# Layer norms written by ScalarE as a scale and a per-row bias, in an adaLN Mamba block on one Trainium2 core

## The chip, the core and the metric

The kernel runs on one core of a Trainium2 chip. The time is the device time in microseconds (us) of one execution; the number that counts is the median of several runs. Engines are named as the profile names them: PE is TensorE (matmuls; PEld are its weight loads), DVE is VectorE, ACT is ScalarE, POOL is GpSimd, and SP is the engine whose queue issues most DMAs. Each engine works through its own queue in order; an instruction that waits holds up all that stand behind it on that engine.

## The reference: what is computed

The input x has 4 batches of 512 rows with 512 features. Six modulation vectors per batch come from a small conditioning input c. The block then computes, in fp32:

```python
mod = (_silu(L0_c) @ L0_wmod).reshape(L0_c.shape[0], 6, 1, -1)
h = _layernorm(x, axis=-1) * (1 + ca) + sa
x = x + ga * _L0_attn_ref(h, ...)
h = _layernorm(x, axis=-1) * (1 + cb) + sb
x = x + gb * _L0_ffn_ref(h, L0_ffn_weight, L0_ffn_bias)
```

`_layernorm` is `(x - m) / sqrt(v + 1e-5)` with the mean m and the variance v of a row. `_L0_attn_ref` is a Mamba2 layer: an input projection, a causal convolution of width 4 with silu for x, B and C, a chunked state-space scan over chunks of 128 rows with 64 heads of 16 features, a gate silu(z), and an output projection. `_L0_ffn_ref` is one 512 x 512 matmul with a weight that is reduced to its signs and one scale per output.

## The kernel before

**Tiling.** The 2048 rows are worked on in 8 "halves" h of 256 rows (two to a batch), each in two chunks c of 128 rows. A half has a front and, per chunk, four units (h, c, gp) of 16 heads, and a tail.

**Front of a half.** `load_x` (L75) brings two tiles of 128 x 512. `f_norm` (L307) normalises them with `layer_norm` (L289) under the name a0 to a7; the result is written over the tiles. `f_hT` (L335) turns them on TensorE (`turned_x`, L325, matmuls phT at L330) and ScalarE applies the modulation (L347) into hT. `f_dt` (L353) computes the time steps, mostly on VectorE, and writes sums, exponentials and reciprocals to DRAM. `f_B`, `f_C`, `f_x` run projections (matmuls at L434), a ScalarE step (L450), three VectorE taps of the convolution (L454), tanh on ScalarE (L458) and a VectorE product (L459). `f_z` projects the gate (L434, pp_z; ScalarE L516 and L520, VectorE L522). `f_turned_sums` (L415) turns the sums (pn, L419 to L427).

**A unit.** SP's queue loads the sums of its heads, broadcast (L541, L542). ScalarE takes 16 exponentials of 128 x 128 (L549). VectorE multiplies them by the masked product of C and B (gm L621, L625). TensorE multiplies with x (py, L212 and L215), VectorE and GpSimd add the rest (L666, L671 or L674, L672) and multiply by the gate (L675), and GpSimd prepares the next state (xd, L679).

**Tail of a chunk.** `tail1` (L729): 8 matmuls po (L739) with wout, then on VectorE the gate (L742), the sum with x (L743) into x2, `layer_norm` under the name f{h}_{c} from x2 into t, and on GpSimd the addition of the bias row to x2 (L745). `tail2` (L751): four transposes ph (L757) and four ScalarE activations h (L759). `tail3` (L765): the feed-forward matmuls pf (L775), VectorE L777 and L778, and the store.

**Layer norm** (L289). For each tile VectorE takes the statistics (L295, L296), adds epsilon to the variances (L297); GpSimd raises them to the power of -0.5 (L298), and VectorE computes (t - mean) times rs in one instruction per tile (L300). The a norms have two tiles, the f norms one.

**Start.** `f_first` (L311) does a0 and the first modulation rows. In the first half the kernel also loads the late modulation weights and works them out (`late_mods`, L233, VectorE L243 to L260, with two rows of gates stored over SP's queue at L262), loads wout over the same place (L265), and loads the feed-forward weight in four pieces fw (L272), whose sums and signs VectorE (L274, L277) and ScalarE (L278) take.

**Order.** The lists FRONT, FIRST and SECOND and the steps of the tails fix in which order the program states its work: per step first the fronts, then the tails, then the unit's matmuls and the loads and exponentials of the unit two ahead. The framework's scheduler then makes each engine's queue from it at build time, by order of statement and by when it thinks an instruction's inputs are there. `issue_after` and `glued` pin some matmuls. PSUM tiles with the tag "mm" share 5 places, which the projections, the transposes and the tails take in turn.

Of the kernel before, what the change touches and what calls it, by code (L numbers as in the profile page):

```python
# [11 lines left out]
F32 = mybir.dt.float32  # L12
AF = mybir.ActivationFunctionType
ALU = mybir.AluOpType
AX = mybir.AxisListType
PSUM = bass.MemoryType.PSUM
P = 128
# [23 lines left out]
def adaln_mamba_block(  # L41
# [15 lines left out]
    nc = tc.nc  # L57
# [13 lines left out]
    wk = ctx.enter_context(tc.tile_pool(name="wk", bufs=2))  # L71
# [27 lines left out]
    mhalf = keep.tile([P, 2], F32, name="mhalf")  # L99
# [189 lines left out]
    def layer_norm(tiles, name, into=None):  # L289
        n = len(tiles)  # L290
        st = wk.tile([P, n, 6], F32, tag=f"st{n}", name=f"st_{name}")
        mv = wk.tile([P, n, 2], F32, tag=f"mv{n}", name=f"mv_{name}")
        rs = wk.tile([P, n], F32, tag=f"rs{n}", name=f"rs_{name}")
        for j, t in enumerate(tiles):
            nc.vector.bn_stats(st[:, j, :], t)  # L295
            nc.vector.bn_aggr(mv[:, j, :], st[:, j, :])  # L296
        nc.vector.tensor_scalar(rs, mv[:, :, 1], EPS, None, ALU.add)  # L297
        nc.gpsimd.tensor_tensor(rs, rs, mhalf[:, :n], ALU.pow)  # L298
        for j, t in enumerate(tiles):
            nc.vector.tensor_scalar(  # L300
                into[j], t, mv[:, j, 0:1], rs[:, j : j + 1], ALU.subtract, ALU.mult
            )


# [2 lines left out]
    def f_norm(h):  # L307
        H[h]["xn"] = xs_of.pop(h)
        layer_norm(H[h]["xn"], f"a{h}", H[h]["xn"])
# [419 lines left out]
    def tail1(h, c):  # L729
        b = h // HPB  # L730
        x2 = tails[h, c]
        po = ps.tile([P, DM], F32, tag="mm", name=f"po_{h}_{c}")
        last = (h, c) == (NHALF - 1, 1)
        for g in range(NKI):
            if last and g == NKI - 2:

                with tc.issue_after(last_po.ins):
                    tail2(h, 0)
            last_po = mm(po, H[h]["z"][g // 2][:, g % 2, c * CH : (c + 1) * CH], wout[:, g, :],  # L739
                         start=(g == 0), stop=(g == NKI - 1))  # L740
        t = wk.tile([P, DM], F32, tag="t", name=f"t_{h}_{c}", bufs=1)
        nc.vector.tensor_mul(t, po, gates[b][:, 0, :])  # L742
        nc.vector.tensor_add(x2, x2, t)  # L743
        layer_norm([x2], f"f{h}_{c}", [t])
        nc.gpsimd.tensor_add(x2, x2, gates[b][:, 2, :])  # L745
        tails[h, c] = (x2, t)
        if last:
            with tc.issue_after(last_po.ins):
                tail3(h, 0)
# [156 lines left out]
```

## Time and profile before

| what | value |
|---|---|
| median of 3 runs | 733.64 us (733.6 to 734.45) |
| the profiled execution | 737.38 us |
| its span in the profile | 735.7 us |
| mean granted clock of TensorE | 0.993 |
| instructions | 15007 |

The profile is of one execution, whose time is the span and 1.68 us around it. A line of the list of instruction groups gives the line number, engine, operation, written and read tiles with their shape, the count, the busy time in us and the mean duration of one in ns, then the engine's idle time just before them and what ended most of it. A line of a timeline gives the start, the duration, the engine, the line and the operation, and in brackets the idle time before it and its releaser. The durations of some groups that bear on the change:

| line and engine | what | count | mean ns of one |
|---|---|---|---|
| L295 DVE | statistics of an f tile | 16 | 688 |
| L296 DVE | their mean and variance | 16 | 171 |
| L297 DVE | variance plus epsilon, f (a) | 16 (8) | 143 (222) |
| L298 POOL | power, f (a) | 16 (8) | 560 (1055) |
| L300 DVE | the norm applied, x tiles | 16 | 654 |
| L745 POOL | bias row added to x2 | 16 | 1342 |
| L549 ACT | an exponential into decay | 960 | 395 |

### The profile page before, as it was taken

To read this page: it belongs to the slowest core of one execution; us is meant where nothing else is said; L and a number is where in the kernel's file an instruction comes from. 1 tells how busy PE (TensorE), PEld (TensorE's weight loads), DVE (VectorE), ACT (ScalarE), POOL (GpSimd) and SP (SyncE) were. 2 spreads that over 40 slices of the span, in tenths; PEclk is the share of its full clock that TensorE was granted. 3 is DMA by queue.
4 is the path that set the end of the run, shared out by engine and by line. 5 is a ranking of instruction groups with operands and counts; after the bars stand their busy time and mean duration, and the time that the engine had idled before them with its cause. 6 is when DMAs were issued, how large, how long until landed. Compare 5 with 4: busy or idle time off the path is not lost.

```text
span 735.7 us, 15007 instructions
## 1 busy us (share of the span) xinstructions
PE 700.4 (95%) x5196; PEld 500.8 (68%) x5196; DVE 599.5 (81%) x1170; ACT 522.0 (71%) x1507; POOL 254.8 (35%) x297
## 2 busy tenths in 40 slices
PE   6999979899999999999999999999999999999997
PEld 3786746666677666677677666776667866677754
DVE  3869888876998678986899768996799867996995
ACT  2467658748696697785976787865968768788941
POOL 4021323444243332343223342433414332333652
PEclk9999989999999999999999999999999999999999
DMA  8991693535555256444644256552564537457720
GB/s 279 328 291 41 204 208 85 135 98 142 127 132 144 63 155 137 102 115 102 159 116 130 53 116 168 142 137 53 140 132 114 130 86 176 116 150 151 142 69 29
DMA packets 119067, 99.24 MB, mean 135 GB/s; under 512 B 73984, under 2 KB 97152, under 8 KB 118992
## 3 DMA queue, kind: packets, MB, share of 16 engines
q1 hardware_dynamic: 117808, 96.39, 52.3%
q0 software_dynamic: 896, 1.38, 0.7%
q8 instruction: 41, 0.67, 0.4%
q10 hardware_dynamic: 288, 0.52, 0.2%
q14 instruction: 34, 0.28, 0.1%
HBM read 92.47 MB, written 5.79 MB: 134 GB/s over the span
## 4 chain that ended last, share of the span: by engine, by line
PE 65%; ACT 16%; DVE 9%; DMA 4%; issue 4%; POOL 1%; SPq 1%; ACTq 0%; DVEq 0%; POOLq 0%
PE po L739 14%; PE pp_x L434 11%; PE pp_z L434 10%; ACT decay L549 9%; PE pp_C L434 7%; PE pp_B L434 5%; PE pf L775 3%; PE py L212 2%; PE py L215 2%; DVE decay L625 2%; ACT h L759 2%; DVE u_x L454 2%; DMA fw<-in_ffn_w 2%; ACT win L549 2%; PE gy L215 2%
## 5 line engine op out<-in xcount | busy, mean ns | idle before, releaser
L549 ACT ACTIVATE decay<-decay,st 128x128 f32<-128x128 f32 x960 | 293.9, 395 | 4.2 <-DMA decay<-sums_d 3.7
L625 DVE SCALAR_TENSOR_TENSOR decay<-decay,gm 128x1024 f32<-128x1024 f32 x120 | 160.8, 1341 | 50.3 <-ACT decay L549 47.2
L434 PE MATMUL pp_x<-hT,win 128*128 128x259 f32 x512 | 120.7, 390 | 7.3 <-DVE u_C L454 7.3
L434 PE MATMUL pp_z<-hT,win 128*128 128x256 f32 x512 | 118.1, 383 | 0.0
L434 PEld LDWEIGHTS pp_x<-hT,win 128*128 128x128 f32 x512 | 96.9, 193 | 25.2 <-ACT decay L549 7.7
L739 PE MATMUL po<-wout,z 128*128 128x512 f32 x256 | 113.8, 595 | 0.0
L434 PEld LDWEIGHTS pp_z<-hT,win 128*128 128x128 f32 x512 | 94.3, 189 | 16.3 <-issue 3.5
L675 POOL TENSOR_TENSOR z<-yt,z 128x256 f32<-128x256 f32 x62 | 62.9, 1015 | 76.1 <-DVE yt L674 57.8
L454 DVE SCALAR_TENSOR_TENSOR u_x<-pp_x,cw,u_x 128x256 f32<-128x256 f32 x192 | 83.6, 474 | 1.3 <-ACT u_x L450 0.7
L739 PEld LDWEIGHTS po<-wout,z 128*128 128x128 f32 x256 | 47.5, 190 | 53.1 <-issue 52.4
L672 POOL TENSOR_TENSOR yt<-yt,xs 128x256 f32<-128x256 f32 x46 | 41.4, 899 | 106.3 <-DVE yt L671 78.6
L507 POOL TENSOR_TENSOR xs<-u_x,rr 128x512 f32<-128x512 f32 x32 | 42.7, 1334 | 79.2 <-DVE u_x L459 61.3
L516 ACT ACTIVATE uz<-pp_z,zb 128x256 f32<-128x256 f32 x64 | 27.5, 470 | 59.0 <-PE pp_z L434 59.0
L215 PE MATMUL py<-decay,xpad 128*32 128x128 f32 x1680 | 66.3, 276 | 0.0
L434 PE MATMUL pp_B<-hT,win 128*128 128x259 f32 x256 | 63.5, 396 | 2.7 <-ACT decay L549 1.9
L434 PE MATMUL pp_C<-hT,win 128*128 128x259 f32 x256 | 59.6, 384 | 1.1 <-DVE u_x L454 1.1
L775 PE MATMUL pf<-bwT,h 128*128 128x512 f32 (+1 forms) x136 | 59.0, 578 | 1.4 <-ACT h L759 1.3
L434 PEld LDWEIGHTS pp_B<-hT,win 128*128 128x128 f32 x256 | 47.4, 193 | 14.5 <-ACT decay L549 3.1
L450 ACT ACTIVATE u_x<-pp_x,cb,cw 128x256 f32<-128x256 f32 x64 | 35.3, 560 | 30.5 <-PE pp_x L434 30.4
L434 PEld LDWEIGHTS pp_C<-hT,win 128*128 128x128 f32 x256 | 47.8, 189 | 9.4 <-PE pn L424 1.4
L679 POOL TENSOR_TENSOR xd<-xpad,st 128x256 f32<-128x256 f32 x48 | 34.1, 727 | 55.8 <-PE pst L215 28.3
L212 PE MATMUL py<-decay,xpad 128*32 128x128 f32 x240 | 47.4, 279 | 3.2 <-issue 2.2
(157 smaller groups left out, 1080.9 us busy)
## 6 DMA issues: line engine op xcount, KB each, us to landing
decay<-sums_d SPq DMA_DIRECT2D x120, 256.0 KB
decay<-sums_d SPq DMA_DIRECT2D x120, 128.0 KB
rr<-r_d SPq DMA_DIRECT2D x64, 128.0 KB
e<-e_d SPq DMA_DIRECT2D x96, 64.0 KB
win<-in_w_inT SPq DMA_DIRECT2D x4, 1024.0 KB
xr<-in_x SPq DMA_DIRECT2D x16, 256.0 KB
res<-o SPq DMA_DIRECT2D x15, 256.0 KB
x<-in_x SPq DMA_DIRECT2D x14, 256.0 KB
```

The source lines that it names most:

```text
L212: first = products[0]()
L215: product()
L434: last = mm(pm, win[:, k, col : col + P], H[h]["hT"][:, k, lo:], start=(k == 0), stop=(k == NK - 1))
L450: nc.scalar.activation(u[:, j, :], pm[:, KS - 1 :], AF.Identity, bias=cb[:, t : t + 1], scale=cw[:, t, KS - 1 : KS])
L454: nc.vector.scalar_tensor_tensor(u[:, j, :], pm[:, k : k + T], cw[:, t, k : k + 1], u[:, j, :], ALU.mult, ALU.add)
L507: nc.gpsimd.tensor_tensor(xs, xc, rr, ALU.mult)
L549: nc.scalar.activation(ets[r][:, i, :], ets[r][:, i, :], AF.Exp, bias=H[h]["st"][:, hd : hd + 1], scale=-1.0)
L625: nc.vector.scalar_tensor_tensor(ets[r], ets[r], 1.0, bc_mid(gm[:, r, :], HPG), ALU.min, ALU.mult)
L672: ew.tensor_add(t, t, xs)
L675: ew.tensor_mul(zg, t, zg)
L739: last_po = mm(po, H[h]["z"][g // 2][:, g % 2, c * CH : (c + 1) * CH], wout[:, g, :], start=(g == 0), stop=(g == NKI - 1))
L775: mm(pf, h2[:, k, :], bwT[:, k, cols], start=(k == 0), stop=(k == NK - 1))
```

## The change

In `layer_norm` the norm a0 keeps the former way. For all other norms the sum (t - mean) rs is written as rs t + (-mean rs): VectorE negates the means into a new small tile nm (its tag has the pool's two buffers), GpSimd multiplies nm by rs after the power, and ScalarE writes each tile as an Identity activation with rs as per-row scale and nm as per-row bias. Nothing else is edited.

```diff
         nc.vector.tensor_scalar(rs, mv[:, :, 1], EPS, None, ALU.add)
+        if name == "a0":
+            nc.gpsimd.tensor_tensor(rs, rs, mhalf[:, :n], ALU.pow)
+            for j, t in enumerate(tiles):
+                nc.vector.tensor_scalar(
+                    into[j], t, mv[:, j, 0:1], rs[:, j : j + 1], ALU.subtract, ALU.mult
+                )
+            return
+
+        nm = wk.tile([P, n], F32, tag=f"nm{n}", name=f"nm_{name}")
+        nc.vector.tensor_scalar(nm, mv[:, :, 0], -1.0, None, ALU.mult)
         nc.gpsimd.tensor_tensor(rs, rs, mhalf[:, :n], ALU.pow)
+        nc.gpsimd.tensor_mul(nm, nm, rs)
         for j, t in enumerate(tiles):
-            nc.vector.tensor_scalar(
-                into[j], t, mv[:, j, 0:1], rs[:, j : j + 1], ALU.subtract, ALU.mult
+            nc.scalar.activation(
+                into[j], t, AF.Identity, bias=nm[:, j : j + 1], scale=rs[:, j : j + 1]
             )
```

## The prediction

> **What bounds the kernel now.** I read the page first (busy time, the 40 slices, the chain), then the list of waits, then TensorE's timeline for its gaps, and last the timelines of the engines around each layer norm.
>
> ```profile
> PE 700.4 (95%) x5196; PEld 500.8 (68%) x5196; DVE 599.5 (81%) x1170; ACT 522.0 (71%) x1507; POOL 254.8 (35%) x297
> ...
> PE 65%; ACT 16%; DVE 9%; DMA 4%; issue 4%; POOL 1%; SPq 1%; ACTq 0%; DVEq 0%; POOLq 0%
> ```
>
> TensorE is busy for 95% of the span and holds 65% of the chain that ended last. Added up over its timeline, the gaps before a matmul come to 31.7 us, 6.2 of them ahead of the first matmul and 5.4 in one piece at 94.05 us. So no edit on VectorE or ScalarE can win more than a part of these gaps, and work added to either costs only where TensorE already waits for that engine or nearly does. The chain holds ScalarE for 16% and VectorE for 9%, so the engine that gets the work is the one that sets the end more often.
>
> The layer norms show in the waits. The columns are the time waited in all, the number of waits, the longest:
>
> ```profile
> ACT uz L516 <- PE pp_z L434: 59.0, 15, 9.1
> ...
> POOL xr L745 <- DVE t L300: 6.8, 11, 0.7
> ...
> DVE t L300 <- POOL rs_f L298: 12.8, 16, 1.4
> ```
>
> VectorE's queue stands 0.8 us on average (12.8/16) behind GpSimd's pow before each L300 of a feed-forward row; and ScalarE has long idle stretches, but they lie where it waits for the z projection, not everywhere.
>
> **The change, part by part.** Changed are the norms a1 to a7 (two tiles each) and the 16 norms of feed-forward rows (one tile each): 30 L300 instructions leave VectorE, and 30 activations, 23 tiny multiplies on VectorE (nm = -mean) and 23 tiny multiplies on GpSimd (nm times rs) come. The rows that price them (mean ns of one after the bar):
>
> ```profile
> L516 ACT ACTIVATE uz<-pp_z,zb 128x256 f32<-128x256 f32 x64 | 27.5, 470 | 59.0 <-PE pp_z L434 59.0
> L450 ACT ACTIVATE u_x<-pp_x,cb,cw 128x256 f32<-128x256 f32 x64 | 35.3, 560 | 30.5 <-PE pp_x L434 30.4
> L300 DVE TENSOR_SCALAR t<-xr,mv_f,rs_f 128x512 f32<-128x512 f32 x16 | 11.5, 719 | 12.8 <-POOL rs_f L298 12.8
> L278 ACT ACTIVATE sw<-sw,alpha 128x512 f32<-128x512 f32 x4 | 2.9, 723 | 3.0 <-DVE sw L277 3.0
> ```
>
> *The activation*: L278 is the same function, shape and memory with a per-row scale: 723 ns. L450 differs from L516 in a per-row scale beside the per-row bias, 90 ns. So 723 + 90 = 0.81 us each, 30 x 0.81 = 24.4 us more ScalarE busy time. Neighbours overlap: eight exponentials of 395 ns take 2.44 us together, 0.305 each, 0.09 less than one alone; so an activation takes 0.81 - 0.09 = **0.72 us** of a busy queue.
>
> *VectorE*: L300 has a median of 546 ns (719 is the mean, stretched where GpSimd works beside it). Both L300 groups are 11.5 + 9.8 us busy; less a0's two (1.6) that is 19.7 us out, up to 16.2 us of waits out with them (12.8 for the rows, 3.4 for x). In come 16 x 143 + 7 x 222 ns = 3.8 us by the rows of L297, the same operation and shapes. These stand behind L297, so the pow starts no later.
>
> *GpSimd's multiply* is not in the trace. From below: the 128x2 memset of L100, 92 ns. From above: the pow of the same shape, 558 ns. A tensor-tensor of L672 takes 0.72 us for 256 columns and one of L745 1.28 us for 512 where nothing disturbs them, which leaves 0.17 us for no columns; I take 0.2 us. L745 now waits for the activation instead of L300 and comes some 0.5 us later; behind it on GpSimd stand yt L672, z L675 and xd L679, on an engine with 65% idle.
>
> The new wait is that of the activation on GpSimd. Behind it on ScalarE's in-order queue stand the exponentials L549, u L450, th L458, h L759. TensorE waits for h (PSUM is handed on), VectorE for the exponentials.
>
> Now by place. **Norms f of the second 128 rows of a half** (six places: 165, 251, 338, 425, 512, 598 us): ScalarE idles before uz L516, for example 6.29 us until 253.24. The pow there ends at 251.64; plus 0.2 and 0.81 gives 252.7, before 253.24. Cost 0. **a2 to a7**: the two activations push ScalarE by 1.4 us and idle stretches of about 6 us follow at once; the transposes of x come 20 us later. Cost 0. If the order took that cover away, the price would be that of the next group.
>
> **Norms f of the first 128 rows**, in ScalarE's busiest stretch. At 292 us:
>
> ```profile
> 292.04 0.55 DVE L300 TENSOR_SCALAR t<-xr,mv_f,rs_f 128x512 f32<-128x512 f32 x1 [1.39 <-POOL rs_f L298]
> ...
> 292.56 1.20 ACT L450 ACTIVATE u_x<-pp_x,cb,cw 128x256 f32<-128x256 f32 x2
> ...
> 296.52 1.48 ACT L759 ACTIVATE h<-ph,modT 128x128 f32<-128x128 f32 x4
> ...
> 298.06 2.02 PE L434 MATMUL pp_B<-hT,win 128*128 128x259 f32 x8 [0.24 <-ACT h L759]
> ```
>
> ScalarE has no gap from 290.2 to 298.4, and TensorE waits for h at its end. What is put into that queue ahead of h comes out on TensorE. The stall of 1.39 us that VectorE loses can reappear on ScalarE: none of it if the activation stands behind the eight exponentials, all of it plus 0.2 if ahead. I take 0.3 us, nearer to none, since the exponentials there cover most of it; so d = 0.72 + 0.3 = **1.0 us** per such place (ends: 0, when it lands in a gap, and 1.7).
>
> The sum:
> - 292, 465, 638 us, alike: 3 x 1.0 = +3.0 (0 to 5.1).
> - 206 and 379: here the chain runs through L300, and TensorE waits 0.57 for u_x L454, which goes; but pn L419 waits for h, and would end at 213.40 + 1.0 instead of 213.97: +0.43 each, +0.9 (-1.1 to +2.3).
> - 552: TensorE waits 0.44 for h: +1.0 (0 to 1.7).
> - 685: ScalarE is full from 679 to 706 with the exponentials of the last half and thz L520 holds up VectorE and then py: +1.0 (0 to 1.7).
> - 118: the queue of VectorE is full until 138 and two gaps, 0.78 and 1.94, wait for it. It gains 0.42 of stall and 0.46 of work, loses 0.14: -0.75 (-1.0 to 0). ScalarE's results are there 1.5 us early or more, which hides d.
> - a1, 74 us: TensorE waits 1.02 for x. Two activations behind uz, xpad, thz: +0.5 (0 to 1.3).
> - The gap of 5.36 at 94: VectorE stands 1.49 and 0.32 us for fw, issued at 82.26 in SP's queue, which earlier stood 3.7 us for ab L260; that stood behind a1's L300. Without these, ab is some 2.8 us earlier, then fw and the gap: at most the 1.81 that VectorE waits, I take -1.5 (-1.8 to 0).
> - The end, 726.5: multiply 0.2, activation 0.81 for 0.55: +0.46 (0.4 to 0.9). At 718.8 matmuls of po hide it.
>
> 3.0 + 0.9 + 1.0 + 1.0 - 0.75 + 0.5 - 1.5 + 0.46 = **+4.6 us**. The profiled execution took 737.38 us, 1.68 more than its span of 735.7, and would be 742.0. The median of the runs, 733.64, is 3.7 below it; the same step there gives **738.2 us**.
>
> A rule speaks against the change itself: the Trainium skill, "ScalarE: Activation LUTs", section "Rules for kernel authors", gives add and multiply to VectorE, not ScalarE. The rows bear it out for one instruction (0.81 against 0.55). By the rule alone each of the eight saturated places and the end would pay 0.26, 2.4 us in all; the trace says that the price is not the difference but the place in the queue.
>
> **The rivals.**
> - *VectorE's relief decides* (faster). The place is VectorE's queue around the first-row norms and a1; the price is what the sum grants at its lower ends: -1.8, -1.0, -1.1 and the end's +0.4 = -3.5, **730.1 us**. It decides from the point where d falls below about 0.2 us, that is, where the build places the activations into ScalarE's short waits for u_C and pp_x (1.19 us before 289.69). For it: 36 us leave VectorE's queue (19.7 + 16.2), and ScalarE's waits for th_C on u_C, 24.2 us, are VectorE's lateness. Against: TensorE's gaps that VectorE ends hold some 15 us, most of them before 140 us.
> - *A wash*: ScalarE's 200 us of idle time takes all 30, and gains and losses cancel: **733.6 us**. For it: 22 of the 30 sit in idle stretches already.
> - *The stall moves whole*: the build puts the activation ahead of the eight exponentials at each saturated place, ScalarE stands for the full lag of the pow, GpSimd's L745 behind it, and z and yt behind that. Upper ends: 5.1 + 2.3 + 1.7 + 1.7 + 1.3 + 0.9 - 0 = +13, **746.6 us**.
> - That it doesn't do what it says: the instructions do move, but the build orders every queue anew, so places far from any norm may shift by parts of a microsecond either way; the trace can't price that, and the range carries it.
>
> **How the numbers follow.** Forecast 0.48, relief 0.27, wash 0.15, whole stall 0.10. Within 0.2% of 733.64 (1.5 us) is about what can't be told from no change: that is the wash. Slower by more: 0.48 + 0.10 = 0.58; faster by more: 0.27. The forecast's own range is 735.2 to 742. The range for 8 in 10 takes in the relief down to its end, 730.0, and the forecast with the beginning of the whole stall, up to 745.0.
>
> **What would show it.** Right: ScalarE 546 us busy, VectorE about 583, TensorE's still 700; activations of t near 0.81 us, GpSimd's multiply near 0.2; wider TensorE gaps after h L759 near 298, 471, 645 us; an earlier fw and a gap below 4 us near 94. Wrong: the gaps after h unchanged because the activations sit in waits; TensorE's gaps for u_C and u_x gone altogether; or fw no earlier.

## The result and the profile after

| | before | after |
|---|---|---|
| median of the runs beside each other | 734.05 us (733.6 to 735.5, 4 runs) | 756.36 us (755.84 to 757.5, 4 runs) |
| ratio, with its 95% interval | 1 | 1.0303 (1.0283 to 1.0322) |
| profiled execution, its span | 737.38, 735.7 us | 756.03, 754.3 us |
| mean granted clock of TensorE | 0.993 | 0.989 |

The changed kernel is 3% slower, 22 us, where 4.6 us were forecast. 756.36 us lies above the whole range. The two profiled executions are only 18.6 us apart, since the one of before was slower than the median of its kernel. In the kernel after, the lines below the edit move by 11 (L434 is L445, L549 is L560, L759 is L770); the activation is L311, the power L308, GpSimd's multiply L309.

First the page of the kernel after: busy time of each engine, and the shares of the chain that ended last.

```profile
PE 705.6 (94%) x5196; PEld 502.6 (67%) x5196; DVE 583.2 (77%) x1163; ACT 544.1 (72%) x1537; POOL 270.4 (36%) x320
...
PE 59%; ACT 16%; DVE 15%; issue 5%; DMA 3%; SPq 1%; POOL 1%; ACTq 0%; DVEq 0%; POOLq 0%
```

The work moved as it was meant to: ScalarE 522.0 to 544.1 us, VectorE 599.5 to 583.2. But VectorE, with less to do, holds 15% of the chain instead of 9%. TensorE's gaps, added up over its timeline, went from 31.7 to 45.1 us, and its busy time from 700.4 to 705.6; the 13.4 and the 5.2 are the 18.6 us by which the span grew.

The list of groups of the kernel after, by line and shape (busy us, mean ns of one, then the idle time before them and what ended it):

```profile
L311 ACT ACTIVATE t<-xr,nm_f,rs_f 128x512 f32<-128x512 f32 x16 | 13.0, 813 | 56.0 <-POOL nm_f L309 56.0
...
L311 ACT ACTIVATE x<-x,nm_a,rs_a 128x512 f32<-128x512 f32 x14 | 10.6, 811 | 5.6 <-POOL nm_a L309 5.6
...
L309 POOL TENSOR_TENSOR nm_f<-nm_f,rs_f 128x1 f32<-128x1 f32 x16 | 3.7, 232 | 1.3
```

The prices of single instructions came out as forecast: 0.81 us for an activation, 0.23 us for the multiply of one column (0.39 us for the seven of two columns). The list of waits of the kernel after (us in all, times, longest):

```profile
DVE decay L636 <- ACT decay L560: 69.8, 66, 4.1
...
ACT t L311 <- POOL nm_f L309: 56.0, 16, 11.8
...
ACT uz L527 <- PE pp_z L445: 16.1, 14, 2.1
...
POOL xr L756 <- ACT t L311: 8.4, 12, 0.9
```

Two rows are to be read together. ScalarE stands 56 us for nm, but its wait for the z projection fell from 59.0 to 16.1: most of the new wait lies in time that was idle anyway, and 56 is no price. The row that has grown for nothing in return is the first: VectorE stood 47.2 us for the exponentials before, and now stands 69.8.

The lag of TensorE, which is the start of the same matmuls (phT, ph, pf) in the kernel after less that in before, tells where the time goes. It is -1.1 us at 75 us, which is no gain of the change: a control without it (before_ux_first) has -1.3 us there. Then it rises in steps. The same steps are shown for a kernel of the experiments (c6_ux_first) in which only f1_0 to f6_0 are on ScalarE and two activations u_x stand ahead of the second eight exponentials again, as they did in before:

| place | forecast | after | f1_0 to f6_0, pair of u_x ahead |
|---|---|---|---|
| a1, fw gap and f0_0 (75 to 141 us) | +0.5 - 1.5 - 0.75 | +4.1 | (not moved) |
| f1_0, f3_0 (206, 379) | +0.43 each | +3.1, +3.0 | +0.43, +0.43 |
| f2_0, f4_0 (292, 465) | +1.0 each | +2.3, +2.2 | +1.0, +1.0 |
| f5_0 (552) | +1.0 | +2.7 | +0.4 |
| f6_0 and f7_0 (638, 685) | +2.0 | +1.6 | +0.9 (f6_0 alone) |
| second rows, a2 to a7 | 0 | about 0 (-0.4 between 141 and 207 us) | (not moved) |
| the end (f7_1) | +0.46 | +1.2 | (not moved) |

The place at 292 us, shown in the prediction for before, reads so in the timeline of the kernel after (start, duration, engine, line, operation, then in brackets the idle time before and its releaser):

```profile
297.11 0.56 POOL L308 TENSOR_TENSOR rs_f<-rs_f,mhalf 128x1 f32<-128x1 f32 x1
297.75 0.19 POOL L309 TENSOR_TENSOR nm_f<-nm_f,rs_f 128x1 f32<-128x1 f32 x1
297.97 0.81 ACT L311 ACTIVATE t<-xr,nm_f,rs_f 128x512 f32<-128x512 f32 x1 [1.77 <-POOL nm_f L309]
...
303.60 1.00 ACT L461 ACTIVATE u_x<-pp_x,cb,cw 128x256 f32<-128x256 f32 x2
...
304.49 1.48 ACT L770 ACTIVATE h<-ph,modT 128x128 f32<-128x128 f32 x4
...
305.83 2.43 DVE L465 SCALAR_TENSOR_TENSOR u_x<-pp_x,cw,u_x 128x256 f32<-128x256 f32 x6
...
307.93 2.24 PE L445 MATMUL pp_C<-hT,win 128*128 128x259 f32 x9 [1.19 <-DVE u_x L465]
```

ScalarE stands 1.77 us for the product and then works 0.72 us: d, forecast at 1.0, is 2.5 us here and 1.8 to 2.0 at the places like 206 (379 and 552). And the pair of u_x, which in before ran at 292.56, ahead of the second eight exponentials, now runs behind them, just before h. TensorE waits for VectorE's taps on that u_x (the line at 305.83).

### The profile page after: what moved, and what is told of

The parts are those of the page before. It is cut to its first block, busy times and chain, and to the rows that moved or that the text cites. A ratio compares the mean times of both kernels' runs of the same rounds, so it can differ in the third digit from the quotient of the medians.

```text
span 754.3 us, 15035 instructions
## 1 busy us (share of the span) xinstructions
PE 705.6 (94%) x5196; PEld 502.6 (67%) x5196; DVE 583.2 (77%) x1163; ACT 544.1 (72%) x1537; POOL 270.4 (36%) x320
## 4 chain that ended last, share of the span: by engine, by line
PE 59%; ACT 16%; DVE 15%; issue 5%; DMA 3%; SPq 1%; POOL 1%; ACTq 0%; DVEq 0%; POOLq 0%
PE po L750 12%; PE pp_z L445 11%; ACT decay L560 10%; PE pp_x L445 10%; PE pp_C L445 5%; PE pp_B L445 4%; DVE decay L636 4%; PE pf L786 4%; PE py L212 2%; PE py L215 2%; DMA decay<-sums_d 2%; DVE u_x L465 2%; ACT h L770 1%; PE gy L215 1%; PE pa L379 1%
## 5 line engine op out<-in xcount | busy, mean ns | idle before, releaser
L560 ACT ACTIVATE decay<-decay,st 128x128 f32<-128x128 f32 x960 | 294.7, 395 | 2.5 <-DMA decay<-sums_d 1.9
L636 DVE SCALAR_TENSOR_TENSOR decay<-decay,gm 128x1024 f32<-128x1024 f32 x120 | 165.0, 1376 | 70.8 <-ACT decay L560 69.8
L445 PE MATMUL pp_x<-hT,win 128*128 128x259 f32 x512 | 118.4, 384 | 4.1 <-DVE u_C L465 4.1
L445 PE MATMUL pp_z<-hT,win 128*128 128x256 f32 x512 | 118.1, 383 | 0.0
L445 PEld LDWEIGHTS pp_x<-hT,win 128*128 128x128 f32 x512 | 95.0, 189 | 21.4 <-ACT decay L560 3.2
L445 PEld LDWEIGHTS pp_z<-hT,win 128*128 128x128 f32 x512 | 94.3, 189 | 16.3 <-issue 3.1
L683 POOL TENSOR_TENSOR yt<-yt,xs 128x256 f32<-128x256 f32 x46 | 47.0, 1022 | 102.9 <-DVE yt L682 65.0
L445 PE MATMUL pp_C<-hT,win 128*128 128x259 f32 x256 | 63.8, 404 | 5.1 <-DVE u_x L465 5.1
L445 PE MATMUL pp_B<-hT,win 128*128 128x259 f32 x256 | 64.5, 399 | 2.4 <-DVE S L723 2.4
L690 POOL TENSOR_TENSOR xd<-xpad,st 128x256 f32<-128x256 f32 x48 | 39.0, 829 | 67.6 <-ACT xpad L504 42.9
L445 PEld LDWEIGHTS pp_C<-hT,win 128*128 128x128 f32 x256 | 50.9, 202 | 14.8 <-DVE u_x L465 4.0
L445 PEld LDWEIGHTS pp_B<-hT,win 128*128 128x128 f32 x256 | 47.6, 194 | 14.2 <-DVE S L723 3.6
L311 ACT ACTIVATE t<-xr,nm_f,rs_f 128x512 f32<-128x512 f32 x16 | 13.0, 813 | 56.0 <-POOL nm_f L309 56.0
```

The lines of the kernel that those rows point to most:

```text
L445: last = mm(pm, win[:, k, col : col + P], H[h]["hT"][:, k, lo:], start=(k == 0), stop=(k == NK - 1))
L560: nc.scalar.activation(ets[r][:, i, :], ets[r][:, i, :], AF.Exp, bias=H[h]["st"][:, hd : hd + 1], scale=-1.0)
L636: nc.vector.scalar_tensor_tensor(ets[r], ets[r], 1.0, bc_mid(gm[:, r, :], HPG), ALU.min, ALU.mult)
L683: ew.tensor_add(t, t, xs)
L690: nc.gpsimd.tensor_tensor(xd, xg, by_head(H[h]["ed"][:, hd0 : hd0 + HPP]), ALU.mult)
```

## The experiments

Three theories for the 22 us. **The stand**: ScalarE now waits for GpSimd at a place where its queue is full, and carries the activation besides; what is behind comes 1.8 to 2.5 us later. **The order**: the scheduler, given an instruction in another queue, put the other instructions in a new order, and that order costs. **Lateness spread over all 30 norms**, the second rows and the a norms as well. The kernels that narrow it down come first, those that decide last. All ratios are to before on the same chip; the median of before there was 735.6 to 736.4 us, so 0.1% is 0.74 us.

**Which norms: no_c0, c0_only, mix.** The condition that keeps a norm in the former way is widened:

```diff
-        if name == "a0":
+        if name == "a0" or name[0] == "f" and name[-1] == "0":                        # no_c0
+        if not (name[0] == "f" and name[-1] == "0"):                                  # c0_only
+        if name in ("a0", "a1", "f7_1") or name[0] == "f" and name[-1] == "0":        # mix
```

> As the changed kernel, but the eight norms of the first 128 rows of a half (f0_0 to f7_0) stay on VectorE; 22 of 30 activations remain. Theory A (the loss is made in the tails of the first chunks, where ScalarE is full): 735 to 738 us, what is left being a1 near 76 us and the end. Theory B (the loss is spread over all 30 activations, about 0.75 us each): 22/30 of 22 us, so about 750 us.

> Only the eight norms of the first chunks (f0_0 to f7_0) go to ScalarE, all others stay on VectorE. Theory A (loss made in the first chunks' tails): 750 to 754 us. Theory B (0.75 us for each activation): 8 x 0.75, about 740 us.

> ScalarE applies only the norms that fell into its idle stretches: a2 to a7 and f0_1 to f6_1; a0, a1, the first-chunk norms and the last one stay on VectorE. If the loss of the kernel without the first-chunk norms comes from a1 near 76 us and from the end, this is 733 to 738 us, within 0.3% of before. If activations in ScalarE's idle stretches cost too, 739 us or more.

Measured: no_c0 1.0089 (1.0060 to 1.0118), c0_only 1.0270 (1.0236 to 1.0304), mix 1.0008 (0.9995 to 1.0020). The eight norms of first rows alone make nearly the whole loss; the thirteen norms of mix, all in ScalarE's idle stretches, cost nothing that can be told. That excludes the spread lateness. no_c0 differs from mix by a1 and f7_1: its lag is 3.4 us by 141 us and flat after it, where mix has -1.2, so a1 alone makes some 4.7.

**What of a first-row norm: no_pow_act, no_pow_dve, wait_only, work_only.** In the first two, GpSimd's leg is taken out of the chain (VectorE takes a reciprocal, and the square root is left out); in the last two VectorE keeps the norm, and ScalarE gets a tiny activation that only waits for rs, or one of full length that waits for nothing new.

```diff
-        nc.gpsimd.tensor_tensor(rs, rs, mhalf[:, :n], ALU.pow)       # no_pow_act: after, no_pow_dve: before
-        nc.gpsimd.tensor_mul(nm, nm, rs)
+        nc.vector.reciprocal(rs, rs)
+        nc.vector.tensor_mul(nm, nm, rs)
...
+            nc.scalar.activation(dmy, rs, AF.Identity, scale=2.0)                     # wait_only, 128x1
...
+            nc.scalar.activation(                                                     # work_only, 512 columns
+                dmy, ones.unsqueeze(1).to_broadcast([P, 4, P]), AF.Identity, bias=mv[:, 0, 0:1], scale=mv[:, 0, 1:2]
+            )
```

> As the changed kernel, but VectorE works out 1/(v + eps) by a reciprocal and nm as well, in place of GpSimd's power: the square root is left out, so that the activation waits for VectorE alone. To be held against the next kernel, which does the same without the activation. Theory S (ScalarE's queue stands for GpSimd's power): the stall of 1.1 to 1.8 us in front of each t goes, 0.72 us of work stays at eight places, so 4 to 8 us above its own comparison. Theory R (the build orders ScalarE's queue otherwise, two u_x behind eight more exponentials): its order of f2_0, f3_0 and so on is nearly that of the changed kernel, so 15 us or more above its comparison.

> As the kernel before, but VectorE works out 1/(v + eps) by a reciprocal in place of GpSimd's power (the square root is left out); VectorE applies all norms. The comparison for the kernel without the power on ScalarE. VectorE loses its waits of 16.2 us for GpSimd. Both theories: 730 to 734 us, since few of TensorE's gaps wait for VectorE.

> The kernel before (VectorE applies all norms), plus one tiny ScalarE activation of 128x1 per first-chunk norm that reads rs behind GpSimd's power into a tile that nobody reads; eight in all, 0.2 us of work each. The build leaves the order of the u_x and the exponentials as before and puts the tiny activation behind one exponential. Theory S (ScalarE's stand for GpSimd is the loss): 1.1 to 1.8 us lost at seven places, the clock's falls on top, 743 to 750 us. Theory R (reordering) and theory W (the 0.72 us of work): within 2 us of before.

> The kernel before, plus one ScalarE activation of 512 columns per first-chunk norm with a per-row scale and bias that waits for VectorE's mean and variance only, reads a constant and writes a tile that nobody reads: the work without GpSimd and without a reader. Theory W (work in a full queue): 7 or 8 times 0.72, 738 to 742 us. Theory S: the same or less, since nothing stands; well below the kernel with the tiny waiting activation.

Measured: no_pow_act 1.0045 (1.0030 to 1.0060), no_pow_dve 0.9938 (0.9917 to 0.9959), wait_only 1.0069 (1.0046 to 1.0092), work_only 1.0141 (1.0124 to 1.0158). Without GpSimd's leg the change costs 1.1% (1.0045 against 0.9938) instead of 3.0%. It looked as if the stand were the cause. But the two parts by themselves, 5 and 10 us, do not make the 20 of c0_only, neither fell in the range of any theory, and the losses sit elsewhere: work_only loses 4.6 of its 8.8 us of lag at f0_0, where the scheduler had turned over u_B, bwT, th_B and h in ScalarE's queue, and 0.6 at each place like 206. wait_only, whose queue keeps the order of before but for the tiny activation, loses 0.3 at f0_0 and 0.2 to 1.5 elsewhere.

no_pow_act tells more. At 206, 379 and 552 us it has another order than the changed kernel (one of the pair of u_x ahead of the second eight exponentials, one behind). At 292, 465 and 638 it has the changed kernel's, with th_x ahead of the second eight and the pair behind them, but the activation doesn't stand. ScalarE's timeline of no_pow_act:

```profile
292.53 0.81 ACT L311 ACTIVATE t<-xr,nm_f,rs_f 128x512 f32<-128x512 f32 x1
...
294.42 0.62 ACT L469 ACTIVATE th_x<-u_x 128x512 f32<-128x512 f32 x1
294.94 2.44 ACT L560 ACTIVATE decay<-decay,st 128x128 f32<-128x128 f32 x8
297.28 1.00 ACT L461 ACTIVATE u_x<-pp_x,cb,cw 128x256 f32<-128x256 f32 x2
```

TensorE's lag rises by 0.9 us at 292 and at 465, where the changed kernel loses 2.3 and 2.2, and at the other four places it doesn't rise. So the new order without the stand is not dear; what it costs together with the stand, these four kernels do not say.

**The norm stated one step later: defer_c0.** c0_only, with the activation and the addition of L745 stated in the next step of the program, so that the wait falls behind more work.

```diff
-        layer_norm([x2], f"f{h}_{c}", [t])
-        nc.gpsimd.tensor_add(x2, x2, gates[b][:, 2, :])
+        put = layer_norm([x2], f"f{h}_{c}", [t])
...
+            todo = steps.setdefault(now[0] + DEFER, [])
```

> Only the eight first-chunk norms on ScalarE, as in the kernel that lost 20 us, but the activation and GpSimd's addition of the bias row are stated one step later, so that the build puts them behind all eight exponentials and some u_x. Theory S: the power is long done there, the stand is gone and 0.72 us of work is left, 738 to 743 us. Theory R (any reordering around u_x and h): 750 us or more again, since th_x and u_x change places here too.

Measured: 1.0198 (1.0176 to 1.0219). ScalarE doesn't stand at any of the six places any more, and 14.6 us of loss stay: now ph waits for a late t (one gap of 2.94 us at 291), and f2_0, f4_0 and f6_0 lose 4.0 to 5.5 us each where f1_0 and f3_0 lose nothing. A price that changes hands like this is no proof of either theory.

**One place at a time: a1_only, f00_only, f10_only, best.** The condition names one norm; best has the norms of mix, and f0_0, f3_0 and f5_0 one step later: 16 norms, not the 18 of its expectation.

```diff
+        if name != "a1":        # a1_only;  "f0_0": f00_only;  "f1_0": f10_only
```

> Only the norm a1 (the first prefetched pair of x tiles, at 74 us) goes to ScalarE. Forecast of step 1: +0.5 us (0 to 1.3), 734 to 735 us. Theory of the stand (in the trace of after the two activations stand 5.56 us for GpSimd's product ahead of eight exponentials, hT follows late, and TensorE's gap before pa L379 is 3.52 us): +3.4 to +4.7 us, 738 to 741 us beside a kernel before of 735.5 to 736.5, nearly all of it before 100 us. Theory that only norms f of first rows cost: no difference.

> Only the norm f0_0 (at 118 us) goes to ScalarE. Here the build keeps it BEHIND eight exponentials and turns u_B, bwT, th_B and h over in ScalarE's queue. Theory of the order (the 4.6 and 5.9 us that two earlier kernels lost at this place with t or a dummy come from the turned order and not from the wait): +4 to +6 us, 740 to 742 us. Theory of the wait (only a wait ahead of exponentials costs): 0 to +1 us, 736 to 737. Forecast of step 1: -0.75 us.

> Only the norm f1_0 (at 206 us) goes to ScalarE; its queue there has the order of the changed kernel (t behind one exponential, the pair u_x behind the second eight). Forecast of step 1: +0.43 us (-1.1 to +1.3). If each place costs what it showed in the changed kernel, +2.3 to +2.9 us, 738 to 739 us beside 735.5 to 736.5; if those losses were made further up and only came out here, 0 to +0.5 us. The fall of the granted clock to 0.50 near 220 us comes with it if the two gaps there make it, and stays away if it was left over from earlier ones.

> ScalarE applies only the norms that cost nothing there: a2 to a7, f0_1 to f6_1, and, stated one step later, f0_0, f3_0 and f5_0 (18 norms in all); the rest stay on VectorE. Theory of the wait and the order: the idle-stretch norms give 0 (the kernel with these alone was 1.0008 of before), f0_0 one step later gave 2.6 us at its place, f3_0 1.1 and f5_0 between -0.3 and +0.8: 732 to 735 us, a ratio of 0.994 to 1.000. If the gain at f0_0 was made by something else in that kernel (its a norms stayed on VectorE), 735 to 738 us.

Measured: a1_only 1.0068 (1.0045 to 1.0091), f00_only 1.0053 (1.0036 to 1.0069), f10_only 1.0040 (1.0019 to 1.0062), best 1.0035 (1.0021 to 1.0049). Each place costs what it showed in the changed kernel: f10_only has a lag of -0.34 us before 206 us and 2.44 behind it, flat until 640 us (there, where nothing was edited, another 1.1 us appears; places far from an edit can differ that much between two kernels). best was to reach 732 to 735 us and took 738.86: what f0_0 gained one step later in defer_c0 did not come again, and f5_0 and the end cost 1 us each. Why isn't settled.

a1 in the timeline of a1_only:

```profile
73.23 1.52 ACT L311 ACTIVATE x<-x,nm_a,rs_a 128x512 f32<-128x512 f32 x2 [5.56 <-POOL nm_a L309]
...
74.66 2.43 ACT L560 ACTIVATE decay<-decay,st 128x128 f32<-128x128 f32 x8
...
78.70 1.91 ACT L358 ACTIVATE hT<-phT,modT 128x256 f32<-128x256 f32 x4
...
79.31 0.69 PE L379 MATMUL pa<-hT,win 128*64 128x128 f32 x4 [3.52 <-ACT hT L358]
```

ScalarE stands 5.56 us ahead of eight exponentials that before had done in that time; uz, xpad, thz and hT come behind them, and TensorE waits 3.52 us for hT, where before it waited 0.22.

**Stand against order: c6_only, dup, c6_ux_first, before_ux_first.** c6_only moves only f1_0 to f6_0. dup leaves t to VectorE and adds at the same six places an activation of 512 columns that reads the same rows and rs and writes a tile that nothing reads. c6_ux_first is c6_only with priority for the two activations of the u_x pair; before_ux_first is its control.

```diff
+        if name not in ("f1_0", "f2_0", "f3_0", "f4_0", "f5_0", "f6_0"):              # c6_only, c6_ux_first
...
+            nc.scalar.activation(dmy, tiles[0], AF.Identity, bias=mv[:, 0, 0:1], scale=rs[:, 0:1])    # dup
...
+            with tc.high_priority(offset=400) if name == "x1" and h > 1 else nullcontext():           # *_ux_first
                 nc.scalar.activation(
                     u[:, j, :], pm[:, KS - 1 :], AF.Identity, bias=cb[:, t : t + 1], scale=cw[:, t, KS - 1 : KS]
                 )
```

> ScalarE applies only f1_0 to f6_0; the queue at f0_0, a1 and the end is that of before, at the six places that of the changed kernel. If the place prices add up (2.8 to 2.9 for each of f1_0, f3_0, f5_0, 1.5 to 2.3 for each of f2_0, f4_0, f6_0): +13 to +15 us, 749 to 751 us beside 735.5 to 736.5. If the first place's loss in the changed kernel came with losses further up (a1, f0_0): +5 to +10.

> Before, with VectorE still writing t, and at f1_0 to f6_0 an additional activation of ScalarE that reads the same rows and rs, over 512 columns, into a tile that nothing reads: same place behind one exponential, same stand, same work as in the changed kernel, and GpSimd's addition waits for it alike; but of the two u_x only one is put behind the second eight exponentials, not both. If stand and work make the price: nearly that of the kernel with the six real norms, +12 to +15 us. If the turned order of the u_x pair makes most of it: clearly less, +3 to +8 us.

> The six norms f1_0 to f6_0 on ScalarE, at the same place behind one exponential, with the same stand and work, and t needed as before; only the two activations of the u_x pair get priority, so that they stand among the first eight exponentials and no longer behind the second eight. If the turned order makes the 14.7 us of these six norms: +0 to +5 us, 736 to 741 us beside 735.5 to 736.5. If it is the lateness of t, or stand and work: +10 to +15 us, 746 to 751.

> Control: before with the same priority for the u_x pair and all norms on VectorE. Before already has the pair ahead of the second eight exponentials, so both theories expect 0 to -1.5 us, 734 to 736.5 us; if the priority alone wins time, what the kernel with it shows has to be set against this one.

Measured: c6_only 1.0212 (1.0181 to 1.0243), dup 1.0027 (1.0006 to 1.0048), c6_ux_first 1.0053 (1.0036 to 1.0069), before_ux_first 1.0001 (0.9991 to 1.0011). dup stands and works like c6_only, and costs 2 us instead of 15.6, even less than was expected if order makes it. dup leaves t where it was, so the deciding pair is c6_only and c6_ux_first: t on ScalarE in both, behind one exponential in both, ScalarE's six waits for the product 7.8 us in the one and 7.6 in the other. The edit touches the pair of u_x alone; with it the build put th_x back behind the second eight exponentials and changed VectorE's queue. The last h ends 6.9 us after its ph starts at 206 us in both kernels (5.15 in before), so the activation delays h equally. **With the stand in place, the new order makes 1.6% of c6_only's 2.1%, some 11.7 us; with the order mended, stand, work and a later t together make 0.5%.** The priority alone, in the control, gives nothing. The two parts are no sum of independent prices. In no_pow_act the same order without the stand cost 0.9 us each at 292 and 465, where the changed kernel loses 2.3 and 2.2: there the order and the stand make the loss together. At 206, 379 and 552 the new order was never run without the stand.

How it happens is seen at 206 us. The timeline of c6_only:

```profile
203.33 2.43 DVE L465 SCALAR_TENSOR_TENSOR u_x<-pp_x,cw,u_x 128x256 f32<-128x256 f32 x6
204.68 0.81 ACT L311 ACTIVATE t<-xr,nm_f,rs_f 128x512 f32<-128x512 f32 x1 [0.98 <-POOL nm_f L309]
205.40 2.14 ACT L560 ACTIVATE decay<-decay,st 128x128 f32<-128x128 f32 x7
...
207.45 0.61 ACT L469 ACTIVATE th_x<-u_x 128x512 f32<-128x512 f32 x1
207.58 1.22 DVE L636 SCALAR_TENSOR_TENSOR decay<-decay,gm 128x1024 f32<-128x1024 f32 x1 [1.49 <-ACT decay L560]
207.97 2.43 ACT L560 ACTIVATE decay<-decay,st 128x128 f32<-128x128 f32 x8
...
210.30 1.00 ACT L461 ACTIVATE u_x<-pp_x,cb,cw 128x256 f32<-128x256 f32 x2
...
211.20 1.49 ACT L770 ACTIVATE h<-ph,modT 128x128 f32<-128x128 f32 x4
211.77 2.43 DVE L465 SCALAR_TENSOR_TENSOR u_x<-pp_x,cw,u_x 128x256 f32<-128x256 f32 x6
...
212.75 0.33 PE L430 MATMUL pn<-ident,sh 128*128 128x128 f32 x1 [1.62 <-ACT h L770]
```

and that of c6_ux_first:

```profile
204.93 0.81 ACT L311 ACTIVATE t<-xr,nm_f,rs_f 128x512 f32<-128x512 f32 x1 [1.01 <-POOL nm_f L309]
...
205.94 0.55 ACT L462 ACTIVATE u_x<-pp_x,cb,cw 128x256 f32<-128x256 f32 x1
...
206.52 0.48 DVE L466 SCALAR_TENSOR_TENSOR u_x<-pp_x,cw,u_x 128x256 f32<-128x256 f32 x1 [0.50 <-ACT u_x L462]
...
207.56 0.55 ACT L462 ACTIVATE u_x<-pp_x,cb,cw 128x256 f32<-128x256 f32 x1
...
211.45 1.49 ACT L771 ACTIVATE h<-ph,modT 128x128 f32<-128x128 f32 x4
...
212.99 3.77 PE L445 MATMUL pp_C<-hT,win 128*128 128x259 f32 x16 [1.12 <-ACT h L771]
```

VectorE, rid of the norm, does its first six taps at once (203.33) and then has nothing: it stands 1.49 us for the exponentials, because ScalarE, its supplier here, is behind and has put the second pair of u_x last. Those six taps run only from 211.77, where all are in TensorE's way: gaps of 1.62 (h) and 0.51 (u_x) where before had 0.57. With the pair put early, two of the taps run while VectorE would stand, and the gap is 1.12. The relief of VectorE was real, and was turned into idle time of VectorE.

**The whole change with the order mended: most_ux_first, after_ux_first.** The same priority for the pair; most_ux_first keeps a1, f0_0, f7_0 and f7_1 on VectorE (what is left are 19 norms, in 25 activations), after_ux_first is the changed kernel else.

> a2 to a7, f0_1 to f6_1 and f1_0 to f6_0 on ScalarE (25 norms of 30), with the priority for the u_x pair; a1, f0_0 and the last half stay on VectorE. If order is the price: 734 to 739 us (1.000 +/- 0.004); if not: 745 to 751.

> The changed kernel whole, with the priority for the u_x pair. Of its 22 us the six places then give back 10 to 13 if the order is the price; a1 (5.0 alone), f0_0 (3.9 alone) and the end (1 to 2) stay: 743 to 747 us. If the order isn't the price: 755 to 757.

Measured: most_ux_first 1.0063 (1.0046 to 1.0080), after_ux_first 1.0141 (1.0121 to 1.0161). The changed kernel gets 1.6% back, as much as the six norms alone. most_ux_first is a little above the upper end of its forecast, 1.004, and about the sum of c6_ux_first and mix. No kernel here with the full computation beats before: mix and before_ux_first equal it, and only no_pow_dve was faster.

## Why the prediction was wrong

**What held.** The instruction prices (activation 0.81, multiply 0.2 us), the busy times (ScalarE 546 forecast, 544.1 measured; VectorE 583, 583.2), the second-row norms and a2 to a7 at 0 (mix). The rule that the prediction weighed (the Trainium skill, "ScalarE: Activation LUTs", section "Rules for kernel authors": add and multiply on VectorE) fits the outcome, 3% slower. The 0.26 us an instruction that the prediction worked out beside it is not the price: thirteen norms on ScalarE cost nothing that can be told (mix), others up to 5 us, by their place in the queue. TensorE's busy time was to stay at 700 and is 705.6, for a reason in the last section. The gap of 5.36 us near 94 us became two of 2.98 and 1.11, 1.3 less in all; -1.5 was forecast. VectorE's two waits for fw there are gone, as forecast. But in f00_only, where a1 stays on VectorE, the gap is 4.03, so how much of this is a1's is not shown.

**Step that failed first: the order of the queue was taken as given.** The sum put one activation into ScalarE's queue of before and asked what would come later behind it. With the pair of u_x ahead again, its terms for the six places came out almost to the tenth: 206, 379 +0.43 measured and forecast, 292, 465 +1.0, and only 552 was 0.4 instead of 1.0; 4.2 us in all against 4.9. This is in part luck: in that kernel d was 1.7 to 2.5 us at five of the six and not 1.0, and TensorE paid only a part of it. The build did not keep the order, and this, on top of the stand, costs some 12 us. The prediction named it ("the build orders every queue anew") under the rivals, but said that places "far from any norm" may shift "by parts of a microsecond", "and the range carries it". It was the place of the norm itself, by 0.7 to 2.7 us each, always with the same sign. How the scheduler came to it (VectorE, which it thinks free sooner, makes th_x ready sooner, and the exponentials' inputs are there before the stand ends) is only argued.

**Step that failed second: d = 0.72 + 0.3.** The activation "ahead" of the eight exponentials was given 0.10, and 0.3 us, "nearer to none", was taken, "since the exponentials there cover most of it". The activation was put behind one exponential of eight at the six places from 206 to 638 us, and stands 1.0 to 1.8 us. d was 1.8 to 2.5. The upper end of 1.7 was too low even by the prediction's own words: 0.72 of work, the stall of 1.39 and the 0.2 make 2.3. With the pair ahead again, a quarter to two fifths of d reached TensorE; at 206 it had waited 0.57 us for u_x in before anyway. With t on VectorE the stand has two prices: at the six places wait_only, in the order of before, loses 5.3 us of lag, and dup, with one of the pair ahead and one behind, 2.6. Why isn't settled. The rival that comes nearest, "the stall moves whole" (746.6, some 3 us more with 2.3 in place of 1.7), had the place and the stand right, but not the new order that made the stand dear.

**Step that failed third: a1, "Two activations behind uz, xpad, thz: +0.5".** They were put ahead of these three, and of eight exponentials too. Moved alone, a1 costs 1.0068, 5.0 us (3.3 to 6.7), the gain at the fw gap already in it; forecast for both was -1.0.

**Step that failed fourth: f0_0, -0.75.** Alone it costs 1.0053, 3.9 us (2.6 to 5.1). In f00_only the activation hardly stands (0.11 us); the order of u_B, bwT, th_B and h behind it is turned. TensorE's two gaps there of 0.78 and 1.93 us have become, in the timeline of f00_only:

```profile
120.28 0.44 PE L212 MATMUL pst<-xd,bt 128*64 128x128 f32 x1 [2.45 <-DVE u_B L465]
...
132.51 5.42 PE L445 MATMUL pp_x<-hT,win 128*128 128x259 f32 x16 [2.77 <-DVE u_C L465]
```

"ScalarE's results are there 1.5 us early or more, which hides d" was true of the old order only. a1 and f0_0 don't add up: the two make 4.1 us of lag together by 141 us, and a1_only turns the order at f0_0 as well.

**The relief** (0.27) had a base, but not in the applied norm: no_pow_dve, where VectorE still applies it and only GpSimd's leg is gone, is 0.6% faster than before.

Put together from the ratios: the order at six places, given the stand, 1.6%, stand, work and late t there 0.5%, a1, f0_0 and the end some 0.9% (after_ux_first less c6_ux_first), of 3.0%.

## What to carry to other kernels

Where a scheduler builds the queues, an operation that is moved to another engine is priced twice: by what it puts into the queue, and by the order that the build then chooses for its neighbours; so the new queue is to be looked at before any sum is trusted, and one line of priority can give back much of a loss (here 12 of 22 us). Ask who feeds the engine that is relieved: here it was the engine that was given the work, and VectorE's relief turned into waits. An operation whose inputs come by a round trip over a third engine belongs where the receiving queue is idle: there thirteen norms were free, and elsewhere they cost up to 5 us apiece.

## What the runs showed of the hardware

TensorE's busy time rose by 5.2 us though it had nothing more to do, mostly since matmuls ran at a lower granted clock behind some gaps: 16.4 us of its busy time lie in four stretches with a clock of 0.50, in before 8.5 us in two. It isn't the size of the gap alone that decides. f10_only and c6_only have the same two gaps before pp_C (1.62 and 0.5 us). TensorE's timelines of f10_only, first, and of c6_only:

```profile
215.28 3.74 PE L445 MATMUL pp_C<-hT,win 128*128 128x259 f32 x16 [0.50 <-DVE u_x L465]
...
220.52 3.70 PE L786 MATMUL pf<-bwT,h 128*128 128x512 f32 x8 [1.06 <-DVE u_B L465]
```

```profile
213.96 5.42 PE L445 MATMUL pp_C<-hT,win 128*128 128x259 f32 x16 [0.51 <-DVE u_x L465]
```

Busy time by stretches of c6_only (us of the stretch, busy time of the five engines, then the granted clock in the third column from the end):

```profile
214.00:216.00 2.00, 2.00 (x6) 1.66 (x7) 1.77 (x5) 2.00 (x7) 0.00 (x0) 0.62 0.54 174
216.00:218.00 2.00, 2.00 (x6) 1.52 (x6) 1.81 (x2) 2.00 (x8) 1.27 (x1) 0.52 0.00 0
```

In f10_only the same stretch has a clock of 1.00. The Trainium skill, "TensorE: Matmul & The Clock Gate", Part 1, puts the fall after an idle window of some 3.4 us whose phase runs free of the program. That the same gaps bring the fall in one kernel and not in another agrees with a free phase; but here gaps of 1.6 and 0.5 us with 0.7 us of matmuls between them were enough for it in c6_only, though neither is near 3.4 us. The phase itself no trace here shows.

And the fall costs less than it looks. pp_C takes 1.7 us longer in c6_only, but f10_only then waits 1.06 us for u_B, a wait that c6_only no longer has: the lag that the place leaves is 2.8 us in f10_only and 3.2 in c6_only. The other places say the same. The kernel after has the fall at 206 and 379 us and not at 552, where it waits 1.06 us for u_B instead, and its lag rises by 3.1, 3.0 and 2.7 us; c6_only has no fall at 379 and 552, and loses 2.8 at each. So a fall costs 0.3 to 0.4 us there, not 1.7: the slow matmuls run while the next input is late anyway, and the 5.2 us of busy time cannot simply be added to the gaps as a cause of their own.
